# Two decoder layers with adaptive LayerNorm on one core: scores of layer 1 in two passes, and another order of the first loads

## The chip, the core and the metric

The kernel runs on one core of a Trainium2 chip, in fp32. The metric is the device time of one execution in microseconds (us). Each time is a median of several executions; beside it stands one profiled execution, from which all durations are read.

Names of the engines: PE multiplies matrices (PEld are its weight loads), DVE is the vector engine, ACT the activation engine, POOL the general engine, SP issues most transfers (DMA). PE writes its results to PSUM, which has 8 banks of 512 columns here.

## The reference, cut to what matters

The input `x` has 8 sequences of 512 tokens with 256 features. Both layers are of the form below; the two modulations come from small vectors `c` of each sequence.

```python
mod = (_silu(c) @ wmod).reshape(8, 6, 1, -1)          # shift, scale, gate for attention; the same for the FFN
sa, ca, ga, sb, cb, gb = (mod[:, k] for k in range(6))
ga, gb = ...                                          # sign(g) * max(|g|, 0.25)
h = _layernorm(x) * (1 + ca) + sa
x = x + ga * attn(h)
h = _layernorm(x) * (1 + cb) + sb
x = x + gb * ffn(h)
```

Layer 0 attends with a delta rule, a recurrence over the 512 tokens with a 16x16 state for each of the 16 heads (q, k, v are projections with silu; q and k are normalized, beta is a sigmoid). Its FFN sends each token to the best of 8 experts of width 1024. Layer 1 is causal softmax attention with a relative bias, and a weighted mixture of 8 linear experts:

```python
att = q @ k.T / 4 + rel_emb[bucket(i - j)]            # 16 heads of 16 features, causal
y = softmax(att) @ v @ W_proj.T + b_proj
w = softmax(h @ gate_w + gate_b); w = w * (w >= 0.1); w = w / sum(w)
out = sum_e w[:, e] * (h @ expert_w[e] + expert_b[e])
```

## The kernel before

Tokens are cut into four tiles of 128 positions (`NT` = 4); a tile holds the positions of all 8 sequences.

**Setup.** SP loads the constants, then for both layers `cT` and the whole modulation matrix `wm` (1.5 MB each, L107). PE makes shift and scale (L119, both branches) and the gates (L136), DVE forms the gates (L144 to L151), and they are written to DRAM (`mod_d`, L157). The relative bias becomes strips in DRAM (L161 to L169): `strips` (loaded in `load_strips`, L1069) later holds, for each query of a tile and each head, the negative bias of all distances, with 1e30 where the mask cuts.

**Layer 0.** `front(i, at)` makes tile i ready for the scan: `stats(p)` loads tokens of two sequences and takes their statistics (L415 to L424), `normal` and `project(b)` normalize, transpose (L209), project (L447, L451) and apply silu (ACT, L455 to L461), `squares` reduces (L465), `roots` and `scales` form sigmoid, roots and products (POOL, L489), and `heads` transposes K and V to one head per partition (PE L499, ACT copies L502). It returns pieces with the scan step at which each is to be issued. `scan(i, K, V)` is the recurrence: four DVE instructions for each of 128 positions (L536, L540, L546, L551), one position after the other. `run` puts the pieces between the steps: those of the next tile's front, and those of the tile before (`follow`: the rest of attention, routing, expert weights fetched slot by slot). The front of tile 0 runs ahead of the first scan. After the last scan come routing and experts of tile 3, then layer 1.

**Layer 1.** `prologue(b)` makes qT, kT and v of a sequence; `tail(b)` projects, normalizes and applies the experts. Between them runs a loop of steps n (L1330 on): sequence b = n // 16, column c = (n % 16) // 4 (four heads, one on each quarter of PE's rows), query tile i = n % 4.
- `scores(b, c, i)`: four matmuls of 128 queries by the (i+1)*128 keys so far (L1141). For each head DVE adds the strips and takes the minimum of the row in one instruction (L1150, `sc`, `low`; signs are turned, so the minimum is the highest score), and ACT makes the exponentials with it (L1155, `pr`).
- `turn(b, c, j)`, four steps later: PE transposes the exponentials of key tile j (L1167, 16, 12, 8 or 4 blocks), and ACT and DVE copy two heads each to `prT` (L1174, L1176).
- `weigh(b, c, j, prTs)`, one step after that: four matmuls with v (L1188); at j = 3 DVE copies the sums (L1195, `yTc`). v has a column of ones, so that the sums of the exponentials come along.

The order within a step is written in the loop, and each engine takes its instructions in that order:

```python
step = scores(b, m // NT, m % NT)
with tc.issue_after(step):
    last, turned = turned, None
    turned = b, m // NT, m % NT, turn(b, m // NT, m % NT)
    if last:
        weigh(*last)
    while side and side[0][0] < n + 1:
        side.pop(0)[1]()
```

`side` holds the pieces of `prologue(b + 1)` and `tail(b - 1)`, spread over the steps of a sequence. The experts of a tile (L1297 to L1314) are eight matmuls of 512 columns with two expert products each; DVE accumulates them in turn (L1308, eight for a tile), POOL applies the gate and adds the residual (L1312, L1313).

## Time and profile before

| | |
|---|---|
| median of 3 runs | 2357.68 us (2357.12 to 2360.76) |
| the profiled execution | 2365.3 us, span of its instructions 2363.4 us |
| granted PE clock, mean | 0.863 |
| busy: PE, DVE, ACT, POOL | 1772.9, 1604.5, 1076.1, 642.7 us |
| first instruction of the scan | 98.83 us |
| last instruction of the scan | 1153.1 us |
| first scores of layer 1 | 1456.2 us |
| last scores of layer 1 start | 2251.6 us |

The page cuts the span into 40 slices of 59 us; a digit is the busy share in tenths. Lines of the timeline give start, length, engine, line, operation, output and inputs, the number of instructions merged, and in brackets the idle time before with what ended it. In rows by line, the number after x is the count; then come busy time and the mean of one in ns. Line numbers L are those of the kernel before, and in what is said of the changed kernel those of the changed one.

### The profile page before, as it was taken

Reading aid. Unit: us, or ns where it says so; the run is one execution under the profiler, and the core shown is the slowest. Engines: PE = TensorE matmul, PEld = TensorE weight load, DVE = VectorE, ACT = ScalarE, POOL = GpSimd, SP = SyncE. Lnnn points to the kernel's source line nnn. Section 1 sums busy time; section 2 is a strip of 40 time slices with the busy share of each in tenths; the row PEclk is TensorE's granted clock in tenths of the full one; section 3 lists DMA queues with packets and bytes.
Section 4 is the critical chain, followed back from the end, with each engine's and each line's share of the span. In section 5 each row is a group of like instructions: output and inputs, shape, how many; then the busy total and the mean of one; then the engine's idle time right before and its main releaser. Section 6 shows DMA issues by size and latency. Waiting matters only on the chain. (4 is left out here: it accounts for less than half of the span.)

```text
span 2363.4 us, 32128 instructions
## 1 busy us (share of the span) xinstructions
PE 1772.9 (75%) x10874; PEld 1215.8 (51%) x10874; DVE 1604.5 (68%) x4608; ACT 1076.1 (46%) x2579; POOL 642.7 (27%) x796
## 2 busy tenths in 40 slices
PE   6450006569677896869877797999989999999996
PEld 3220004448566685658656685554545454555543
DVE  2499999988998899899651003666666666665653
ACT  3561004455355543523332235774737374646521
POOL 0211006334472544644336633000000101010111
PEclk8675558579888998879977998999999999999997
DMA  5010000057422682248866883000000000000000
GB/s 187 16 47 0 0 0 6 18 193 269 148 72 96 215 290 80 78 168 311 234 115 202 250 299 101 1 4 21 3 21 4 21 3 21 3 21 6 10 10 9
DMA packets 83444, 209.91 MB, mean 89 GB/s; under 512 B 10248, under 2 KB 59568, under 8 KB 67664
## 3 DMA queue, kind: packets, MB, share of 16 engines
q0 software_dynamic: 28848, 157.42, 19.8%
q1 hardware_dynamic: 54432, 50.45, 7.5%
q8 instruction: 86, 1.41, 0.2%
q14 instruction: 78, 0.64, 0.1%
HBM read 175.10 MB, written 32.74 MB: 88 GB/s over the span
## 5 line engine op out<-in xcount | busy, mean ns | idle before, releaser
L1155 ACT ACTIVATE pr<-sc,low 128x384 f32<-128x384 f32 (+3 forms) x512 | 255.8, 556 | 269.5 <-DVE low L1150 267.9
L943 PE MATMUL ps<-hTs,w 128*128 128x128 f32 x1920 | 245.8, 289 | 51.0 <-ACT hTs L935 32.5
L1150 DVE CUSTOM_DVE_ANT_0 sc<-ps,strips 128x384 f32<-128x384 f32 (+3 forms) x512 | 226.6, 485 | 64.6 <-PE ps L1141 51.6
L943 PEld LDWEIGHTS ps<-hTs,w 128*128 128x128 f32 x1920 | 234.3, 203 | 65.4 <-ACT hTs L935 46.6
L540 DVE TENSOR_REDUCE state<-terms 128x16 f32<-128x272 f32 x512 | 227.3, 444 | 15.7
L961 PE MATMUL ps<-w,act 128*128 128x256 f32 x960 | 223.0, 386 | 18.7 <-DMA w<-in_wrows,idx 15.5
L551 DVE TENSOR_TENSOR state<-state,upd 128x256 f32<-128x256 f32 x511 | 220.6, 432 | 17.2
L1303 PE MATMUL ps<-ew,hTd 128*128 128x512 f32 x512 | 230.7, 604 | 0.0
L546 DVE TENSOR_TENSOR upd<-K,state 128x256 f32<-128x256 f32 x511 | 214.0, 419 | 14.9
L536 DVE TENSOR_TENSOR terms<-state,K 128x256 f32<-128x256 f32 x512 | 214.8, 419 | 12.0
L952 ACT ACTIVATE act<-ps,w 128x128 f32<-128x128 f32 x480 | 137.2, 369 | 184.9 <-PE ps L943 108.2
L1308 DVE SCALAR_TENSOR_TENSOR accd<-ps,wtd,accd 128x256 f32<-128x256 f32 x256 | 123.6, 483 | 120.1 <-PE ps L1303 74.3
L961 PEld LDWEIGHTS ps<-w,act 128*128 128x128 f32 x960 | 181.7, 194 | 44.6 <-issue 16.7
L1167 PE MATMUL ps<-cst,pr 128*128 128x128 f32 x1280 | 192.3, 295 | 12.8 <-DVE low L1150 10.6
L1167 PEld LDWEIGHTS ps<-cst,pr 128*128 128x128 f32 x1280 | 148.7, 149 | 87.1 <-issue 35.9
L1312 POOL TENSOR_TENSOR accd<-accd,bc_g 128x256 f32<-128x256 f32 x32 | 23.3, 729 | 559.3 <-DVE accd L1308 559.3
L1303 PEld LDWEIGHTS ps<-ew,hTd 128*128 128x128 f32 x512 | 95.6, 192 | 119.5 <-issue 106.0
L916 POOL DMA_INDIRECT w<-in_wrows,idx x120 | 117.5, 979 | 122.0 <-ACT act L952 90.3
L1141 PE MATMUL ps<-kT,qTc 32*128 32x384 f32 (+3 forms) x1024 | 132.2, 506 | 11.4 <-DVE v L317 6.8
L570 PE MATMUL ps<-cst,V 128*128 128x128 f32 x64 | 13.0, 385 | 169.4 <-DVE V L542 169.4
L636 POOL TENSOR_TENSOR stk<-stk,cst 128x512 f32<-128x512 f32 x96 | 119.3, 1269 | 19.0 <-ACT stk L635 16.9
L1176 DVE COPY prT<-ps 128x512 f32<-128x512 f32 (+3 forms) x256 | 117.7, 483 | 5.0 <-PE ps L1167 4.5
(238 smaller groups left out, 3024.9 us busy)
## 6 DMA issues: line engine op xcount, KB each, us to landing
hs<-zero SPq DMA_DIRECT2D x4, 1920.0 KB
hslot<-hs SPq DMA_DIRECT2D x60, 128.0 KB
ys<-ysb POOLq DMA_DIRECT2D x60, 128.0 KB, 3.8
xt<-in_x SPq DMA_DIRECT2D x16, 256.0 KB
x<-in_x SPq DMA_DIRECT2D x32, 128.0 KB
strips<-strip_d SPq DMA_DIRECT2D x16, 256.0 KB
out<-accd SPq DMA_DIRECT2D x32, 128.0 KB
wm<-in_wmod SPq DMA_DIRECT2D x2, 1536.0 KB
```

The costliest lines, as they stand in the source:

```text
L536: nc.vector.tensor_mul(term[:, :, :HD], M, K[:, s, :].unsqueeze(1).to_broadcast([P, HD, HD]))
L540: nc.vector.tensor_reduce(delta, term, AX.X, ALU.add)
L546: nc.vector.tensor_mul(upd, K[:, s, :].unsqueeze(2).to_broadcast([P, HD, HD]), delta.unsqueeze(1).to_broadcast([P, HD, HD]),)
L551: yield nc.vector.tensor_sub(M, M, upd).ins
L943: nc.tensor.matmul(ph[:, q * P : (q + 1) * P], w[:, k * FF + f * P : k * FF + (f + 1) * P], hT[:, k, :], start=(k == 0), stop=(k == 1),)
L952: nc.scalar.activation(act[:, f, :], ph[:, q * P : (q + 1) * P], AF.Relu, bias=w[:, 2 * FF + f : 2 * FF + f + 1],)
L961: nc.tensor.matmul(py[:, :D], act[:, f, :], w[:, f * D : (f + 1) * D], start=(f == 0), stop=(f == NFC - 1),)
L1141: made = nc.tensor.matmul(pscs[r][:, :W], qT[rows, g, o, i * P : (i + 1) * P], kT[rows, g, :W], start=True, stop=True,)
L1150: nc.vector.tensor_tensor_reduce(out=sc[:, :W], in0=pscs[r][:, :W], in1=strips[:, n, S - W :], scale=1.0, scalar=3.0e38, op0=ALU.add, op1= ...
L1155: nc.scalar.activation(pr, sc[:, :W], AF.Exp, bias=low, scale=-1.0)
L1167: nc.tensor.transpose(pt[:, (i - j) * P : (i - j + 1) * P], prs[r, i][:, j * P : (j + 1) * P], ident,)
L1303: nc.tensor.matmul(pe, hT[:, k, cols], ew[:, k, e : e + 2, :], start=(k == 0), stop=(k == 1),)
```

## The change

**Setup and layer 0.** The block ahead of layer 0 goes. The modulation matrix is loaded in four parts (layer, branch); the first comes right after the constants, then the tokens of tile 0 (`x_first`, in the room of K), then `wqkv`, then the other three parts and the buckets. Shift and scale of layer 0's attention are made first. The rest of the modulation (`shift_scale`, with ACT copies), the gates (`gate_rows`: ACT copy, four DVE instructions on 8x256, POOL's DMA), the strips (`strip_rows`: now two kinds, POOL's DMAs), the product of the output weights and the loads of the gates become pieces of the first scan, at its steps 2 to 26. The front of tile 1 starts at step 30 of that scan (before: 2). In tile 0, `stats_first` takes all statistics with one square root, `turn(b)` is apart from `project(b)` and ahead of it, `roots` and `scales` run once for all eight sequences, DVE takes some of the products, and DVE makes half of the copies in `heads`.

**Layer 1.** `scores` keeps matmul and reduction and only leaves the minima (`lows`), in columns that the transpose puts at a row of q that meets a constant 1 in k. `highest` (one step later) transposes them (L1305) and subtracts them from q: for i = 3 on DVE from PSUM, otherwise ACT negates and POOL adds. `exps` then multiplies k by q again, the other way round (keys by queries, L1324), DVE adds transposed strips (L1332, `stripsT`, 4 MB loaded when layer 0's room is free) and ACT makes the exponentials in place (L1333). There is no transpose of exponentials and no copy. In the loop the order is `scores`, `highest` of the step before, `weigh` of the step before, side pieces, `exps`. k is kept in two masked copies, v is packed 20 columns a head. In `experts`, DVE accumulates two of the eight products; for the other six ACT scales and POOL adds. The copies `yTc` and `wT` move from DVE to ACT.

The diff, cut to its core:

```diff
+        def load_mod(layer, branch):
+            if branch == 0:
+                nc.sync.dma_start(
+                    cTs[layer], t[f"cT{layer}"].rearrange("(k p) b -> p k b", p=P)
+                )
+            wm = fp.tile([P, 2, 3 * D], F32, tag=f"w{branch}", name=f"wm{layer}{branch}", bufs=2)
+            cols = slice(3 * D * branch, 3 * D * (branch + 1))
+            nc.sync.dma_start(
+                wm, t[f"wmod{layer}"][:, cols].rearrange("(k p) m -> p k m", p=P)
+            )
+            wms[layer, branch] = wm
...
+        def gate_rows(layer, branch):
+            wm = wms[layer, branch]
+            pg = bank()
+            for k in range(2):
+                nc.tensor.matmul(
+                    pg[:B, :D], scs[layer][:, k, :], wm[:, k, 2 * D :],
+                    start=(k == 0), stop=(k == 1),
+                )
+            name = f"{layer}{branch}"
+            g, sign, mag, gt = (
+                fp.tile([B, D], F32, tag=tag, name=f"{tag}_{name}", bufs=2)
+                for tag in ("hslot", "yrow", "ysb", "hTs")
+            )
+            nc.scalar.copy(g, pg[:B, :D])
+            nc.vector.tensor_scalar(sign, g, 0.0, 2.0, ALU.is_ge, ALU.mult)
+            nc.vector.scalar_tensor_tensor(mag, g, -1.0, g, ALU.mult, ALU.max)
+            nc.vector.tensor_scalar_max(mag, mag, 0.25)
+            nc.vector.scalar_tensor_tensor(gt, sign, -1.0, mag, ALU.add, ALU.mult)
+            nc.gpsimd.dma_start(mod_d[f"g{name}"], gt)
...
+        load_mod(0, 0)
+        for p in range(B // 2):
+            nc.sync.dma_start(
+                x_first[:, 2 * p : 2 * p + 2],
+                t["x"][2 * p : 2 * p + 2, :P, :].rearrange("b p d -> p b d"),
+            )
         nc.sync.dma_start(wqkv, t["wqkvT0"].rearrange("(k p) m -> p k m", p=P))
+        shift_scale(0, 0)
+        for layer, branch in ((0, 1), (1, 0), (1, 1)):
+            load_mod(layer, branch)
+        load_buckets()
...
+            def stats_first():
+                mv = room[:, 1, : 2 * B].rearrange("p (b s) -> p b s", s=2)
+                sd, rs, off = (room[:, 1, k * B : (k + 1) * B] for k in (2, 3, 4))
+                for b in range(B):
+                    st = ep.tile([P, 6], F32, tag="sta", name=f"st_first{b}", bufs=2)
+                    nc.vector.bn_stats(st, x_first[:, b, :])
+                    nc.vector.bn_aggr(mv[:, b, :], st)
+                nc.scalar.activation(sd, mv[:, :, 1], AF.Sqrt, bias=ln_eps)
+                nc.vector.reciprocal(rs, sd)
+                nc.vector.scalar_tensor_tensor(
+                    off, mv[:, :, 0], -1.0, rs, ALU.mult, ALU.mult
+                )
+                for p in range(B // 2):
+                    bs = slice(2 * p, 2 * p + 2)
+                    got[p] = x_first[:, bs], rs[:, bs], off[:, bs]
...
+                        ve = nc.vector if i == 0 and which and b % 2 else nc.gpsimd
+                        ve.tensor_mul(view, view, by.unsqueeze(2).to_broadcast([P, NH, HD]))
...
+                    if i == 0 and d0 % 8:
+                        nc.vector.tensor_copy(to, pt.rearrange("p (d t) -> p d t", d=4))
+                    else:
+                        nc.scalar.copy(to, pt.rearrange("p (d t) -> p d t", d=4))
...
+            else:
+                pieces = [
+                    (2, weights0),
+                    (4, lambda: shift_scale(0, 1)),
+                    (6, lambda: gate_rows(0, 0)),
+                    (8, lambda: gate_rows(0, 1)),
+                    (10, lambda: shift_scale(1, 0)),
+                    (12, lambda: shift_scale(1, 1)),
+                    (14, lambda: gate_rows(1, 0)),
+                    (16, lambda: gate_rows(1, 1)),
+                    (18, lambda: strip_rows(0)),
+                    (20, lambda: strip_rows(1)),
+                    (26, load_gates),
+                ]
...
-                parts, more = front(i + 1, 47 if i > 0 else 2)
+                parts, more = front(i + 1, 47 if i > 0 else 30)
...
         def scores(b, c, i):
-            kT, qT, prs = got[b]["kT"], got[b]["qT"], got[b].setdefault(c, {})
+            kT, qT = got[b]["kT"], got[b]["qT"]
             g, o = c // 2, c % 2
             W = (i + 1) * P
             pscs = [bank() for _ in range(4)]
             for r in range(4):
                 rows = slice(32 * r, 32 * r + 32)
                 made = nc.tensor.matmul(
-                    pscs[r][:, :W], qT[rows, g, o, i * P : (i + 1) * P], kT[rows, g, :W],
+                    pscs[r][:, :W], qT[rows, g, o, i * P : (i + 1) * P], kT[rows, g, o, :W],
                     start=True, stop=True,
                 )
+            at = HD * (1 - o)
             for r in range(4):
                 n = 8 * g + 2 * r + o
-                sc = lp.tile([P, S], F32, tag="sc", name=f"sc{b}_{i}_{n}", bufs=4)
-                low = lp.tile([P, 1], F32, tag="low", name=f"low{b}_{i}_{n}", bufs=8)
+                sc = lp.tile([P, S], F32, tag="sc", name=f"sc{b}_{i}_{n}", bufs=1)
                 nc.vector.tensor_tensor_reduce(
                     out=sc[:, :W], in0=pscs[r][:, :W], in1=strips[:, n, S - W :],
-                    scale=1.0, scalar=3.0e38, op0=ALU.add, op1=ALU.min, accum_out=low,
-                )
-                pr = lp.tile([P, W], F32, tag=f"pr{i}", name=f"pr{b}_{i}_{n}", bufs=6)
-                nc.scalar.activation(pr, sc[:, :W], AF.Exp, bias=low, scale=-1.0)
-                prs[r, i] = pr
+                    scale=1.0, scalar=3.0e38, op0=ALU.add, op1=ALU.min,
+                    accum_out=lows[:, o, i % 2, r, at : at + 1],
+                )
             return made.ins
-        def turn(b, c, j):
-            prs = got[b][c]
+        def highest(b, c, i):
+            g, o = c // 2, c % 2
+            pt = bank()
+            nc.tensor.transpose(
+                pt[:, :P], lows[:, o, i % 2].rearrange("p r e -> p (r e)"), ident
+            )
+            q = got[b]["qT"][:, g, o, i * P : (i + 1) * P]
+            if i == NT - 1:
+                nc.vector.tensor_sub(q, q, pt[:, :P])
+                return
+            high = lp.tile([P, P], F32, tag="high", name=f"high{b}_{c}_{i}")
+            nc.scalar.mul(high, pt[:, :P], -1.0)
+            nc.gpsimd.tensor_add(q, q, high)
+        def exps(b, c, j):
+            kT, qT = got[b]["kT"], got[b]["qT"]
+            g, o = c // 2, c % 2
             W = S - j * P
+            pscs = [bank() for _ in range(4)]
+            for r in range(4):
+                rows = slice(32 * r, 32 * r + 32)
+                nc.tensor.matmul(
+                    pscs[r][:, :W], kT[rows, g, o, j * P : (j + 1) * P], qT[rows, g, o, j * P :],
+                    start=True, stop=True,
+                )
             prTs = []
             for r in range(4):
-                pt = bank()
-                for i in range(j, NT):
-                    nc.tensor.transpose(
-                        pt[:, (i - j) * P : (i - j + 1) * P],
-                        prs[r, i][:, j * P : (j + 1) * P],
-                        ident,
-                    )
+                n = 8 * g + 2 * r + o
                 prT = lp.tile([P, S], F32, tag="prT", name=f"prT{b}_{c}_{j}_{r}", bufs=8)
-                if r % 2:
-                    nc.scalar.copy(prT[:, :W], pt[:, :W])
-                else:
-                    nc.vector.tensor_copy(prT[:, :W], pt[:, :W])
+                nc.vector.tensor_add(prT[:, :W], pscs[r][:, :W], stripsT[:, n, :W])
+                nc.scalar.activation(prT[:, :W], prT[:, :W], AF.Exp, scale=-1.0)
                 prTs.append(prT)
             return prTs
...
+                sums = lp.tile([P, D], F32, tag="sumd", name=f"sumd{b}_{i}")
+                nc.scalar.copy(sums, pb[:, :D])
                 acc = lp.tile([P, D], F32, tag="accd", name=f"accd{b}_{i}")
-                nc.scalar.copy(acc, pb[:, :D])
                 for e in range(0, NE, 2):
                     pe = bank()
                     for k in range(2):
...
                             start=(k == 0), stop=(k == 1),
                         )
                     for j in range(2):
-                        nc.vector.scalar_tensor_tensor(
-                            acc, pe[:, j * D : (j + 1) * D], wt[:, i, e + j : e + j + 1], acc,
-                            ALU.mult, ALU.add,
-                        )
+                        part, by = pe[:, j * D : (j + 1) * D], wt[:, i, e + j : e + j + 1]
+                        if (e, j) == (0, 0):
+                            nc.vector.tensor_scalar(acc, part, by, None, ALU.mult)
+                        elif (e, j) == (4, 0):
+                            nc.vector.scalar_tensor_tensor(
+                                acc, part, by, acc, ALU.mult, ALU.add
+                            )
+                        else:
+                            term = lp.tile(
+                                [P, D], F32, tag="term", name=f"term{b}_{i}_{e + j}", bufs=2
+                            )
+                            nc.scalar.activation(term, part, AF.Copy, scale=by)
+                            nc.gpsimd.tensor_add(sums, sums, term)
+                nc.gpsimd.tensor_add(acc, acc, sums)
...
-                last, turned = turned, None
+                if 0 < n <= B * STEP:
+                    b, m = divmod(n - 1, STEP)
+                    highest(b, m // NT, m % NT)
+                if made:
+                    weigh(*made)
+                while side and side[0][0] < n + 1:
+                    side.pop(0)[1]()
+                made = None
                 if NT <= n < B * STEP + NT:
                     b, m = divmod(n - NT, STEP)
-                    turned = b, m // NT, m % NT, turn(b, m // NT, m % NT)
-                if last:
-                    weigh(*last)
-                while side and side[0][0] < n + 1:
-                    side.pop(0)[1]()
+                    made = b, m // NT, m % NT, exps(b, m // NT, m % NT)
```

## The prediction

> **What bounds the kernel now.** I read the slices of the page first, then busy time by stage, then the timeline of the stage that is long.
>
> ```profile
> span 2363.4 us, 32128 instructions
> ...
> PE   6450006569677896869877797999989999999996
> ...
> DVE  2499999988998899899651003666666666665653
> ...
> PEclk8675558579888998879977998999999999999997
> ```
>
> One slice is 59 us. DVE is full from slice 2 to 18 (layer 0's scan) and PE from slice 25 to 38 (layer 1). In between the FFN of the last token tile streams its weights, started by the end of the scan.
>
> ```profile
> 1456.20:2251.60 795.40, 737.72 (x4406) 409.95 (x4410) 513.86 (x1828) 479.95 (x1061) 80.31 (x109) 0.96 0.05 13
> 98.80:1152.50 1053.70, 651.89 (x4314) 524.43 (x4315) 960.13 (x2436) 424.43 (x1077) 387.57 (x469) 0.79 0.35 119
> ```
>
> These rows give, for two stretches, the length, then the busy time of PE, weight loads, DVE, ACT and POOL, then PE's clock. In layer 1, PE is busy 93% and DVE 65%; in the scan DVE is busy 91%. So three things set the end: when the scan starts (98.8 us), its DVE time, and PE's order in layer 1. Four steps of layer 1 on PE:
>
> ```profile
> 1775.51 1.97 PE L1167 MATMUL ps<-cst,pr 128*128 128x128 f32 x16 [0.16 <-ACT prT L1174]
> 1777.40 0.43 PE L1188 MATMUL ps<-prT,v 128*32 128x128 f32 x8
> ...
> 1779.65 0.71 PE L1141 MATMUL ps<-kT,qTc 32*128 32x256 f32 x8
> 1780.29 1.53 PE L1167 MATMUL ps<-cst,pr 128*128 128x128 f32 x12
> 1781.75 1.06 PE L1188 MATMUL ps<-prT,v 128*32 128x512 f32 x8
> 1782.75 1.13 PE L313 MATMUL ps<-wqkv,hTc 128*128 128x256 f32 x4
> ...
> 1785.11 0.93 PE L1141 MATMUL ps<-kT,qTc 32*128 32x384 f32 x8
> ...
> 1790.18 1.20 PE L1141 MATMUL ps<-kT,qTc 32*128 32x512 f32 x8
> ```
>
> A step is scores (L1141), transposes of the exponentials (L1167), weighing of the *previous* step's transposes (L1188), then side work (here L313 and what follows). Between the transposes of a step and their weighing lie its side work, the next scores and the next transposes: the copies L1174 and L1176 have some 5 us, and PE hardly ever waits for them. From the start of scores to the first side matmul the four steps take 3.57, 3.10, 2.92 and 3.25 us: **12.84 us for one c**, of which there are 32.
>
> **Layer 1: the steps after.** In the built program PE's order becomes: transposed scores of step n (L1324), scores of n+1 (L1285), one transpose of minima (L1305), weighing of n (L1345), side work, transposed scores of n+1. Weighing now needs what was made just before it: four DVE adds (L1332) and four exponentials (L1333), with only one set of scores as cover; behind the waiting L1345 stand the side work and the next transposed scores, so all of PE. The chain, for widths 512, 384, 256, 128:
> - first result after the matmuls start: 1.16, 0.95, 0.74 (first L1150 after the L1141 starts above: 1791.34, 1786.06, 1780.39), and 0.63 (1456.24 to 1456.87);
> - three more adds, priced as the reductions L1150, which also read PSUM and strips (start to start 0.60, 0.47, 0.345, 0.21): 1.80, 1.42, 1.04, 0.63; the last add's own time 0.69, 0.55, 0.42, 0.29;
> - hand-overs, an estimate: 0.1; the last exponential (L1155 by shape) 0.72, 0.61, 0.50, 0.40;
> - the last weighing, two passes, each as long as one of L1303 (7.06 us for 16 of width 512): 0.90, 0.67, 0.45, 0.25.
>
> Sums: 5.4, 4.3, 3.25, 2.3, or **15.2 us for one c**, against 12.84: +2.4 us x 32 = **+76 us**. If the weighing's two passes of the last tile lay wholly beside other matmuls, it would be 1.1 less for a c: +40.
>
> What PE alone would need: 12.84, less the transposes (start to start 1.89, 1.46, 1.08, 1.04), plus a second set of scores (0.60, 0.64, 0.86, 1.13), plus four transposes at 0.2: 11.4 us. So PE's own work does get shorter, by 1.4 us for a c; it doesn't get to use it.
>
> The other engines, for one of 8 batches. DVE: adds 16 x (0.60+0.47+0.345+0.21) = 26 us and 4 subtractions at 0.3 come; copies (73 us in 550 us, five batches: 14.6), 24 accumulations L1308 at 0.48 (11.6) and the copies of yTc and wT (3.5) go: about -2.5 us. ACT: 24 terms at 0.38, yTc 2.3, negations 12 x 0.25, wT 0.6 and second halves of kT 2.8 come, 12.1 of copies go: +5.7 of 110 us, with ACT at 60% hidden behind PE; uncovered it would be +45 in all. POOL gets 28 additions at 0.73 in expert pieces: with the two old ones nine for a tile, 6.6 us beside PE's 7.7 us for a tile (2341.13 to 2348.82), hidden; where ACT's last term waits for POOL, up to 1 us for each of 32 tiles. The 12 additions of q on POOL have a step of time. The square roots: 15 visits with two table loads of 1.28 us each now stand in the queue ahead of exponentials that PE waits for; from 0 to 15 x 2.9 = 43; I take +10, since the second load can lie beside the adds. At the start, the second strips wait for the last multiplication with the gates (1456 us) and their first quarter, 1 MB, for some 5 us at the 177 GB/s of that stretch, beside the first four scores (SP issues all 32 loads of them ahead of the next batch's tokens, which have until step 6); then the minimum, its transpose and subtraction stand ahead of the first exponentials: +4. At the end ACT and POOL finish the last tile in place of two accumulations: +2 (4 additions of 0.73 less 0.96).
>
> PE will wait 1 us a step, up to 2.3 us; what is its clock then? After a wait of 3.94 us at 1767 us the next scores took 2.09 us instead of 1.20; after one of 1.13 us at 1796.5 us the sixteen transposes took 2.20 instead of 1.97. I price it at 0, by the nearer row; above it, the row of the last 112 us has a clock of 0.89 with PE busy 81%: some 78 us of PE work for a batch x 8 x (0.96/0.89 - 1) = +49. [...]
>
> [...]
>
> **The start.** The scan's first instruction is at 98.83 us. Before it:
>
> ```profile
> 10.60 6.96 PE L119 MATMUL ps<-sc,wm 128*128 128x8 f32 x32 [10.60 <-DMA wm<-in_wmod]
> ...
> 34.18 0.69 PE L209 MATMUL ps<-cst,xna 128*128 128x128 f32 x2 [5.14 <-ACT xna L206]
> ...
> 90.53 3.68 PE L499 MATMUL ps<-cst,qk 128*128 128x128 f32 x16 [10.64 <-POOL qk L489]
> ...
> 98.83 0.38 DVE L532 TENSOR_TENSOR terms<-state,V 128x128 f32<-128x128 f32 x1 [13.47 <-ACT V L502]
> ```
>
> After: 0.39 MB of constants, 0.79 of modulation, 1.05 of tokens, 0.80 of wqkv on one queue, at the 221 GB/s of the first 20 us and 2.5 us before the first lands: modulation 7.8, tokens 12.6, wqkv 16.2 us. Statistics are 0.51 us for each batch, all but the last pair ahead of the last tokens; with root, normalizing and transposes the first projection starts at 16.5 rather than 35.4. A batch costs PE 1.98 + 1.08 + 0.38 = 3.44 us at the fast durations, 3.78 + 2.02 + 0.69 = 6.5 at the slow ones that follow waits; eight of them, one to two slow: 32.5, so to 49 (before 5.8 us for each, with six changes of tables between). From the last projection to the scan it was 18.4 us. POOL's K products now stand after four others and not after eight (-2.5), ACT and DVE share the copies (-1), one reciprocal is twice as wide (+1): 16, with one reduction ahead of it: scan start at 66 to 67. **-32 us**; bounds -24 (tokens in 1 KB rows at half the rate) and -38 (all batches fast).
>
> In the scan DVE gets 16 operations on 8x256 (the 8x512 rows are 0.41, 0.67, 0.41, 0.68; I take two thirds, 1.4 for a gate) and 0.75 for the output weights: **+6**, nothing hides it, as DVE is the bound there; not below +3. The rest (small matmuls, ACT copies, POOL's DMAs of gates and strips, SP's two gate loads) finds engines that are idle half the time; the next tile's front moves from step 2 to 30 and ends at 79 of 128. What follows the scan hangs on its end, so the -26 goes through to layer 1.
>
> **Sum.** +76 +10 +4 +2 -32 +6 = +66 us. The profiled execution took 2365.3 us (span 2363.4), 7.6 above the median of 2357.7; I carry the difference over to the median: **2424 us**. Its own range: 2375 (overlapped last weighing, no root stalls) to 2495 (part of the clock, roots and POOL at their upper ends).
>
> **Rivals.**
> - *The chain is covered, and PE's shorter work counts* (faster). Place: the wait ahead of L1345. Against it: the built order, and DVE's 0.60 us for each add. For it: 15.2 is a sum of parts of which the first result and the last weighing may overlap more. It decides at (26 - 16)/32 = 0.3 us above 12.84, so 13.1 us for a c; fully covered, 11.4 x 32 gives -46 - 26 + 6: 2292 us. Chance 0.22, spread from 2285 to 2353.
> - *PE's clock falls too*, with table loads on top: +49 and more, 2475 to 2530. For it the rows of 1767 us; against it that waits of 1 us left durations alone. Beyond 2495: 0.07.
> - *The first loads don't come earlier*, because tokens and modulation share the engines: -24 in place of -32, 2432; inside the range. 0.08.
>
> The forecast has 0.63, all within 2353 to 2495. The range 2310 to 2495 leaves out some 0.1 below and 0.07 above. A difference of 0.2% is about what a measurement can tell from none: faster 0.22, same 0.03, slower 0.75.
>
> **What would show it.** Right: a scan start near 67 us; in layer 1 PE idle ahead of L1345, put down to ACT's prT (L1333), of 0.5 to 2 us in each step, PE busy under 90%, steps of 6.8 us rather than 6.26. Wrong: PE busy 95% with steps under 6.1 us; or waits that stand at L1324 (for q from POOL) or L1305; or a clock under 0.92.

## The result and the profile after

The changed kernel takes 2499.0 us (median of 4 runs, 2495.06 to 2505.87); the kernel before, beside it, 2359.2 us. The ratio is 1.059, with a 95% interval of 1.0555 to 1.0625: slower by 140 us, where the forecast was slower by 66. The profiled execution took 2505.9 us.

The slices of the page after:

```profile
span 2503.8 us, 32578 instructions
...
PE   5142065696778777689678779999899898989996
...
DVE  3999999889977998993300176646464656465631
...
PEclk8676576798889997799789879999999999999997
```

DVE fills up one slice earlier; PE is at 8 or 9 tenths in layer 1 as before, and its clock stays at 9 there. By these digits nothing is wrong with PE. The stages, as before: length, then busy time of PE, weight loads, DVE, ACT and POOL, then the clock. They are layer 1 from the first to the last scores, the rest of it, the scan, and what lies between scan and layer 1:

```profile
1436.20:2377.30 941.10, 859.94 (x4282) 406.17 (x4283) 551.25 (x1923) 474.68 (x1085) 242.78 (x371) 0.94 0.07 15
2377.30:2503.80 126.50, 100.80 (x322) 44.71 (x318) 29.76 (x96) 46.14 (x108) 58.17 (x81) 0.86 0.03 10
64.66:1126.70 1062.04, 656.85 (x4355) 526.06 (x4354) 963.86 (x2457) 427.33 (x1087) 390.18 (x475) 0.80 0.35 120
1126.70:1436.20 309.50, 241.04 (x1654) 205.98 (x1654) 54.92 (x148) 102.58 (x309) 143.85 (x169) 0.87 0.68 201
```

and the end of layer 1 in the kernel before:

```profile
2251.60:2363.40 111.80, 90.83 (x326) 45.52 (x322) 50.45 (x134) 21.09 (x49) 17.39 (x24) 0.89 0.03 10
```

The scan starts 34 us earlier and layer 1 starts 20 us earlier; the steps of layer 1 take 941 us where they took 795, and the end 126.5 where it took 111.8. Two steps on PE (start, length, engine, line, operation, operands, number, and in brackets the idle time before with its releaser):

```profile
1828.14 1.14 PE L1324 MATMUL ps<-qTc,kT 32*128 32x512 f32 x8
1829.11 0.67 PE L1285 MATMUL ps<-kT,qTc 32*128 32x256 f32 x8
1830.73 0.33 PE L1305 MATMUL ps<-cst,lows 128*128 128x128 f32 x1 [0.95 <-DVE prT L1332]
1831.49 2.81 PE L1345 MATMUL ps<-prT,v 128*32 128x512 f32 x8 [0.42 <-DVE prT L1332]
1834.23 1.13 PE L263 MATMUL ps<-wqkv,hTc 128*128 128x256 f32 x4
...
1836.59 0.93 PE L1324 MATMUL ps<-qTc,kT 32*128 32x384 f32 x8
1837.34 1.72 PE L1285 MATMUL ps<-kT,qTc 32*128 32x384 f32 x8
1839.48 0.33 PE L1305 MATMUL ps<-cst,lows 128*128 128x128 f32 x1 [0.43 <-DVE prT L1332]
1839.74 2.12 PE L1345 MATMUL ps<-prT,v 128*32 128x384 f32 x8
1841.79 1.13 PE L263 MATMUL ps<-wqkv,hTc 128*128 128x256 f32 x4
```

The weighing of width 512 takes 2.81 us, where the same eight matmuls took 1.06 before: they stand and wait for one exponential after the other, 0.62 us apart, and the profile counts part of that as busy. So the busy share of PE (91%) hides what it was to show. The cycle of these two steps, from L1324 to the first side matmul (L263), is 6.1 and 5.2 us; 5.4 and 4.3 were forecast. What DVE does meanwhile:

```profile
1829.66 0.43 DVE L125 BATCH_NORM_STATS2 std<-xs 128x6 f32<-128x256 f32 x1 [0.69 <-POOL xs L1404]
1830.00 0.67 DVE L1332 TENSOR_TENSOR prT<-ps,stripsT 128x512 f32<-128x512 f32 x1
1830.59 0.17 DVE L126 BATCH_NORM_AGGREGATE mvd<-std 128x2 f32<-128x6 f32 x1
1830.68 1.85 DVE L1332 TENSOR_TENSOR prT<-ps,stripsT 128x512 f32<-128x512 f32 x3
1832.45 0.41 DVE L1294 CUSTOM_DVE_ANT_0 sc<-ps,strips 128x256 f32<-128x256 f32 x1
...
1833.02 0.42 DVE L1294 CUSTOM_DVE_ANT_0 sc<-ps,strips 128x256 f32<-128x256 f32 x1
...
1833.60 0.42 DVE L1294 CUSTOM_DVE_ANT_0 sc<-ps,strips 128x256 f32<-128x256 f32 x1
```

Two things were not in the forecast. A statistic of the tail (L125, mean and variance of a tile's rows) stands in DVE's queue ahead of the adds and waits there 0.69 us for POOL's xs. And the reductions, 0.42 us long, start 0.575 us apart; before they started 0.345 apart:

```profile
1780.39 0.41 DVE L1150 CUSTOM_DVE_ANT_0 sc<-ps,strips 128x256 f32<-128x256 f32 x1
...
1780.73 0.42 DVE L1150 CUSTOM_DVE_ANT_0 sc<-ps,strips 128x256 f32<-128x256 f32 x1
```

They now all write the one tile `sc` (before: four). The reading, which experiment A tests, is that each waits until the one ahead has written; no row of waits names this.

The start, on PE:

```profile
7.89 3.56 PE L356 MATMUL ps<-room,wm 128*128 128x8 f32 x16 [7.89 <-DMA wm<-in_wmod]
16.61 1.18 PE L148 MATMUL ps<-cst,xna 128*128 128x128 f32 x4 [5.16 <-ACT xna L145]
17.85 3.68 PE L544 MATMUL ps<-wqkv,hT 128*128 128x512 f32 x4
...
57.43 3.68 PE L605 MATMUL ps<-cst,qk 128*128 128x128 f32 x16 [12.37 <-POOL qk L597]
```

and the first instruction of the scan, on DVE:

```profile
64.66 0.38 DVE L646 TENSOR_TENSOR terms<-state,V 128x128 f32<-128x128 f32 x1
```

Modulation at 7.9 us, first projection at 17.9, scan at 64.7: forecast were 7.8, 16.5 and 66 to 67.

### The profile page after: what moved, and what is told of

It is laid out like the page before. It is cut to its first block, busy times and chain, and to the rows that moved or that the text cites. A ratio compares the mean times of both kernels' runs of the same rounds, so it can differ in the third digit from the quotient of the medians.

```text
span 2503.8 us, 32578 instructions
## 1 busy us (share of the span) xinstructions
PE 1895.7 (76%) x10748; PEld 1208.2 (48%) x10748; DVE 1621.8 (65%) x4668; ACT 1085.3 (43%) x2660; POOL 848.1 (34%) x1118
## 5 line engine op out<-in xcount | busy, mean ns | idle before, releaser
L1332 DVE TENSOR_TENSOR prT<-ps,stripsT 128x256 f32<-128x256 f32 (+3 forms) x512 | 219.4, 481 | 126.5 <-PE ps L1324 111.9
L1294 DVE CUSTOM_DVE_ANT_0 sc<-ps,strips 128x384 f32<-128x384 f32 (+3 forms) x512 | 249.1, 487 | 50.3 <-PE ps L1285 5.7
L1333 ACT ACTIVATE prT<-prT 128x256 f32<-128x256 f32 (+3 forms) x512 | 215.7, 467 | 124.5 <-DVE prT L1332 117.6
L1075 PE MATMUL ps<-w,act 128*128 128x256 f32 x960 | 224.5, 388 | 16.7 <-DMA w<-in_wrows,idx 12.6
L1345 PE MATMUL ps<-prT,v 128*32 128x512 f32 (+3 forms) x1024 | 214.3, 470 | 19.1 <-ACT prT L1333 12.2
L1314 POOL TENSOR_TENSOR qTc<-qTc,high 128x128 f32<-128x128 f32 x96 | 43.6, 454 | 498.6 <-ACT high L1313 498.6
L1285 PE MATMUL ps<-kT,qTc 32*128 32x128 f32 (+3 forms) x1024 | 186.9, 495 | 14.0 <-DVE lows L1294 8.7
L1480 POOL TENSOR_TENSOR sumd<-sumd,term 128x256 f32<-128x256 f32 x192 | 139.1, 725 | 171.9 <-ACT term L1479 165.9
L1479 ACT ACTIVATE term<-ps,wtd 128x256 f32<-128x256 f32 x192 | 84.8, 471 | 164.4 <-DVE accd L1470 78.5
L1285 PEld LDWEIGHTS ps<-kT,qTc 32*128 32x128 f32 x1024 | 103.7, 200 | 75.8 <-DVE prT L1332 25.5
```

The costliest lines, as they stand in the source:

```text
L1075: nc.tensor.matmul(py[:, :D], act[:, f, :], w[:, f * D : (f + 1) * D], start=(f == 0), stop=(f == NFC - 1),)
L1285: made = nc.tensor.matmul(pscs[r][:, :W], qT[rows, g, o, i * P : (i + 1) * P], kT[rows, g, o, :W], start=True, stop=True,)
L1294: nc.vector.tensor_tensor_reduce(out=sc[:, :W], in0=pscs[r][:, :W], in1=strips[:, n, S - W :], scale=1.0, scalar=3.0e38, op0=ALU.add, op1= ...
L1332: nc.vector.tensor_add(prT[:, :W], pscs[r][:, :W], stripsT[:, n, :W])
L1333: nc.scalar.activation(prT[:, :W], prT[:, :W], AF.Exp, scale=-1.0)
L1345: nc.tensor.matmul(yT[32 * r : 32 * r + 32, j * P :], v[:, j, (4 * c + r) * VW : (4 * c + r) * VW + 32], prTs[r][:, :W], start=(j == 0), s ...
```

## The experiments

Four candidates for the time lost in layer 1: **A**, the spacing of the reductions; **B**, the chain add, exponential, weighing that PE waits for; **C**, the experts' sum on ACT and POOL; **F**, the statistics in DVE's queue. In all runs "layer 1" is the time from the first scores to the end in the profiled execution: 907.2 us before (795.4 + 111.8), 1067.6 after (941.1 + 126.5). Each is from one execution; the old layer 1 took 907.2 and 905.7 us in two kernels, so a difference of a few us tells little. Ratios are to the kernel before, run beside each on the same chip. A wait given for a line is that of its matmuls and their weight loads together, as the view of the line has it; PE may be at work on others during part of it.

| kernel | ratio, 95% interval | layer 1, us |
|---|---|---|
| before | 1 | 907.2 |
| changed | 1.059 [1.0555, 1.0625] | 1067.6 |
| new start, old layer 1 | 0.9875 [0.983, 0.992] | 905.7 |
| A: two scratch tiles | 1.045 [1.038, 1.051] | 1043.3 |
| B: side work first | 1.044 [1.039, 1.050] | 1044.8 |
| C: experts' sum on DVE | 1.050 [1.045, 1.055] | 1057.1 |
| F: statistics behind the adds | 1.050 [1.046, 1.054] | 1050.1 |
| A + B | 1.025 [1.023, 1.028] | 985.0 |
| A + B + C | 1.011 [1.009, 1.013] | 965.6 |
| A + B + C, second pass a step later | 1.017 [1.013, 1.021] | 968.1 |
| A + C, weighing a step later | 1.008 [1.005, 1.011] | 967.7 |
| A + B + C + F | 1.000 [0.997, 1.003] | 942.7 |
| changed, no adds in the second pass | 1.024 [1.021, 1.027] | 994.7 |
| A + B + C, no adds | 0.983 [0.978, 0.987] | 901.0 |

**The start alone.** Setup and layer 0 of the changed kernel, with `prologue`, `scores`, `turn`, `weigh`, the experts and the loop as they were before (here against the changed kernel):

```diff
-                nc.vector.tensor_add(prT[:, :W], pscs[r][:, :W], stripsT[:, n, :W])
-                nc.scalar.activation(prT[:, :W], prT[:, :W], AF.Exp, scale=-1.0)
+                if r % 2:
+                    nc.scalar.copy(prT[:, :W], pt[:, :W])
+                else:
+                    nc.vector.tensor_copy(prT[:, :W], pt[:, :W])
...
-                    made = b, m // NT, m % NT, exps(b, m // NT, m % NT)
+                    turned = b, m // NT, m % NT, turn(b, m // NT, m % NT)
+                if last:
+                    weigh(*last)
```

> The new start of layer 0 (quarter of the modulation first, tokens second, the rest and both strips in scan steps) with layer 1 as it was before. All theories: the scan starts near 65 us in place of 98.8 and ends some 27 us earlier, and a layer 1 that is not changed keeps these 27: 2326 to 2340 us against 2359 before. Nearer to 2359: the start's gain is given back between the scan and layer 1, and the layer 1 of the change costs less than it seems. The distance from this run to the changed kernel (about 165 us if 2333) is what the two-pass scores cost as a whole.

Measured: 2334.6 us, ratio 0.9875, some 30 us gained; layer 1 took 905.7 us, as before.

```profile
1417.00:2210.60 793.60, 736.65 (x4408) 408.79 (x4410) 514.02 (x1828) 479.92 (x1061) 80.17 (x109) 0.96 0.05 13
```

So the start's gain is kept, and the two-pass layer 1 costs 165 us by itself. This version is faster than both kernels, and the fastest here of those that compute the whole reference.

**A: the spacing of the reductions.**

```diff
-                sc = lp.tile([P, S], F32, tag="sc", name=f"sc{b}_{i}_{n}", bufs=1)
+                sc = lp.tile([P, S], mybir.dt.bfloat16, tag="sc", name=f"sc{b}_{i}_{n}", bufs=2)
```

> The changed kernel with two scratch tiles for the reductions in place of one (16 bits wide, so that both fit where one was; nothing reads them). Theory A, spacing: four reductions that write one tile wait for each other, which is 0.23 us each, 512 in all or 118 us of VectorE, and lies on the chain from scores to highs to exponentials: starts of the reductions go back from 0.84/0.70/0.575/0.445 us apart to about 0.60/0.47/0.345/0.21, and the time falls by 50 to 110 us, to 2390 to 2450. Rival B, chain: the wait of the weighing for the exponentials sets the step and the reductions have slack: within 15 us of 2499. Rival C, experts: as B.

Measured: ratio 1.045, layer 1 24 us shorter. Reductions of width 256 on DVE:

```profile
1705.57 0.41 DVE L1294 CUSTOM_DVE_ANT_0 sc<-ps,strips 128x256 bf16<-128x256 f32 x1
...
1705.91 0.42 DVE L1294 CUSTOM_DVE_ANT_0 sc<-ps,strips 128x256 bf16<-128x256 f32 x1
...
1706.25 0.42 DVE L1294 CUSTOM_DVE_ANT_0 sc<-ps,strips 128x256 bf16<-128x256 f32 x1
```

They start 0.34 us apart again and are no shorter themselves, so the second tile did it and not the narrower type; three tiles of 32 bits (in A + B + C) give 0.345 as well. The cause is real; the size was expected at two to four times as much. The 118 us of the expectation count 512 gaps; a batch of four reductions has three, so 88 us at most, and only 24 of them stood in the path while PE waited for the exponentials anyway (117 us ahead of L1345 in both kernels).

**B: the chain's cover.**

```diff
-                if made:
-                    weigh(*made)
                 while side and side[0][0] < n + 1:
                     side.pop(0)[1]()
+                if made:
+                    weigh(*made)
```

> The changed kernel with the side work of a step ahead of the weighing on TensorE, so that about two pieces of it lie beside the way from the adds to the exponentials. Theory B, chain: the 117 us that TensorE waits at L1345 for prT fall below 60, and the time falls by 50 to 120 us, to 2380 to 2450. Rival A, spacing: VectorE is late with the adds by its queue (reductions, then the side's operations), so the wait only moves to the banks (transposes of the highs and the side's matmuls waiting for VectorE's prT): 2470 to 2515. Rival C, experts: as A.

Measured: ratio 1.044, layer 1 23 us shorter. The wait for exponentials ahead of L1345 fell from 117.0 to 19.8 us, more than expected, and layer 1 by less than half of the 50 us that were the least expected. Other waits grew: at the scores (L1285) for banks that the adds free from 26.9 to 63.6 us, and at L1345 itself 20.5 us came in for the experts' terms on ACT (L1479; 1.1 at most in the changed kernel). And PE's clock fell; first the row of all steps, then three stretches:

```profile
1420.10:2341.20 921.10, 806.37 (x4280) 395.42 (x4283) 550.65 (x1923) 473.30 (x1085) 244.77 (x372) 0.87 0.07 16
1540.00:1560.00 20.00, 17.01 (x113) 10.14 (x109) 14.54 (x51) 10.10 (x25) 4.14 (x7) 0.84 0.00 1
1555.00:1560.00 5.00, 5.00 (x16) 3.15 (x19) 3.01 (x11) 1.83 (x5) 0.45 (x1) 0.50 0.00 0
1560.00:1580.00 20.00, 18.52 (x123) 9.34 (x115) 12.49 (x47) 15.49 (x33) 2.36 (x4) 0.98 0.03 8
```

In the 20 us from 1540 on the longest wait of PE was 1.62 us (it ended at 1553.84), and the clock was 0.84; in the 5 us from 1555 on PE was busy throughout and the clock was 0.50. Over all steps it was 0.87, against 0.94 in the changed kernel, where much of PE's waiting lay within the weighing. What lowers the clock there is not shown by these rows.

**C: the experts' sum.**

```diff
...
-                            nc.scalar.activation(term, part, AF.Copy, scale=by)
-                            nc.gpsimd.tensor_add(sums, sums, term)
-                nc.gpsimd.tensor_add(acc, acc, sums)
+                        nc.vector.scalar_tensor_tensor(
+                            acc, pe[:, j * D : (j + 1) * D], wt[:, i, e + j : e + j + 1], acc,
+                            ALU.mult, ALU.add,
+                        )
```

> The changed kernel with the experts' sum on VectorE alone as it was before (8 operations of 0.42 us per tile in place of two, no terms on ScalarE and no sums on GpSimd). Theory C, experts: terms of 0.47 us stand among the exponentials on ScalarE, and GpSimd's sums hand xs to the next batch late: the time falls by 20 to 60 us (2440 to 2480), the tail after the last scores goes from 126 us back to about 113. Rivals A and B: VectorE takes 192 more operations, 80 us busy, and is the engine that is late: the time rises by 5 to 40 us (2505 to 2540), only the tail gains some 12.

Measured: ratio 1.050, some 21 us by the ratios and at the low end of what was expected; layer 1 by itself is 10.5 us shorter, although DVE is busier in it by 90 us. The tail only went from 126.5 to 123.8 us, so that part was wrong: the last tile's sum on ACT and POOL is not what made the end longer. The traces show where most of it lies. In the changed kernel, over several engines:

```profile
1937.14 0.72 POOL L1483 TENSOR_TENSOR accd<-accd,xs 128x256 f32<-128x256 f32 x1
...
1938.33 1.81 SPq L256 DMA_DIRECT2D xs<-x  x4
...
1941.11 0.43 DVE L125 BATCH_NORM_STATS2 stc<-xs 128x6 f32<-128x256 f32 x1 [3.13 <-DMA xs<-x]
...
1943.98 0.69 PE L1387 MATMUL ps<-cst,yc 128*128 128x128 f32 x2 [5.86 <-DVE yc L1377]
```

SP issues the next sequence's tokens (L256) behind the store of an experts' tile (at 1937.89 us), which waits for POOL's sum; DVE stands at their statistic, with `yc` (L1377) behind it in its queue, and PE waits for `yc`. PE's matmuls waited 29.4 us for `yc` in the changed kernel, 20.4 with C, and 21.9 in the kernel before.

**A and B together, then C, then the second pass later.** A + B is both edits; the next adds C (with three tiles `sc` of 32 bits); the last also has

```diff
-                if NT <= n < B * STEP + NT:
-                    b, m = divmod(n - NT, STEP)
+                if NT < n <= B * STEP + NT:
+                    b, m = divmod(n - NT - 1, STEP)
```

> The changed kernel with both edits: two scratch tiles for the reductions, and the side work ahead of the weighing. Alone they took 24 and 23 us from layer 1 (first scores to end: 1067.6 us in the changed kernel, 1043.3 and 1044.8 with the one or the other). Theory A and B together, two causes in one chain: with the side work ahead of the weighing what is left to wait for is VectorE's adds (transposes of the highs and scores wait for banks), and shorter spacing brings just these forward: 50 to 85 us in all, layer 1 at 985 to 1018, 2415 to 2450 us. Rival, one slack counted twice: whichever is cured first leaves the other nothing: 22 to 35 us in all, layer 1 at 1033 to 1045, 2465 to 2480.

> As the kernel with both edits, and the experts' sum back on VectorE (the scratch tiles are then three of 32 bits). Alone the third edit took 10 us from layer 1, and none from its tail. Theory C adds: 8 to 25 us less than with two edits. Rival: with the spacing cured VectorE is what sets the step, and 80 us more of work on it cost 5 to 30 us against the two edits.

> As the kernel with three edits, with the second pass one step later, so that the highs of a c have a step more to reach q before the first exponentials need them. Theory D, the highs' route (transpose, ScalarE's negation or VectorE's subtraction, q) stands in the path once per c: 0.5 to 1 us for each of 32 c's, so 15 to 32 us less than with three edits. Rival: other work stands there already: within 8 us of it.

Measured: A + B took 82.6 us from layer 1 (at the upper end of what was expected), where A and B alone took 24.3 and 22.8. So with the exponentials covered the spacing counts for more: PE's waits for the reductions ahead of L1285, L1305 and L1324 are 34.4 us here and 60.0 in B alone. The expected way, that the adds free their banks sooner, doesn't show: the waits for these were 63.6 us at L1285 and 67.7 at L1305 in B alone, and are 68.8 and 65.6 here. The clock is likely the larger part: it was 0.87 in B alone and is 0.92 here.

```profile
1429.10:2297.30 868.20, 766.14 (x4283) 375.46 (x4284) 524.27 (x1923) 472.58 (x1085) 244.45 (x372) 0.92 0.07 17
```

With PE 806 us busy at 0.87 in B alone, the step to 0.92 is worth 806 x (1 - 0.87/0.92) = 44 us, an estimate; the surplus of both over the sum of each is 35.5. Of the 53 us between the steps of B alone (921.1) and these (868.2), 40 lie in PE's busy time for the same matmuls (806.4 and 766.1), which fits; a part of that can be blocked matmuls that read as busy, and the two were not told apart. C took 19 us more, within what was expected: PE's matmuls waited 33.0 us for `yc` with A + B and 22.1 with C, and the 20.5 us at L1345 for ACT's terms are gone. The second pass a step later did not help (965.6 and 968.1 us, ratios 1.011 and 1.017), so by these runs the way from the minima to q has slack.

**The weighing a step later.** In place of B, with A and C; the tiles for the exponentials become as narrow as their step needs, four sets of them:

```diff
-        side, made = [], None
+        side, made = [], []
...
-                if made:
-                    weigh(*made)
+                if len(made) > 1 or n > B * STEP + NT:
+                    weigh(*made.pop(0))
```

> The changed kernel with two scratch tiles, the experts' sum on VectorE, and (in place of the side work ahead of the weighing) the weighing one step later: the exponentials then have a whole step, since the tiles for them are as narrow as each step needs and so there are four sets. Theory B, chain: another cover for the same wait does what the first did: no wait at L1345 for the exponentials, layer 1 within 20 us of the 965.6 us of the kernel with three edits, 2375 to 2410 us. Rival: the gain of the three edits came from the side work's place between scores and weighing, and not from the wait: layer 1 near 1025 us (1067.6 less 24 less 19), 2440 to 2465 us.

Measured: layer 1 at 967.7 us, 2 us from A + B + C. Another cover for the same wait does the same, so it was the wait and not the place of the side work that B cured.

**Without the adds.** The relative bias and the mask are left out of the second pass:

```diff
-                nc.vector.tensor_add(prT[:, :W], pscs[r][:, :W], stripsT[:, n, :W])
-                nc.scalar.activation(prT[:, :W], prT[:, :W], AF.Exp, scale=-1.0)
+                nc.scalar.activation(prT[:, :W], pscs[r][:, :W], AF.Exp, scale=-1.0)
```

> The changed kernel without the second pass's adds on VectorE: ScalarE takes its exponentials straight from the banks, so the relative bias and the mask are left out of the second pass. Theory B, chain: 512 adds of 0.28 to 0.67 us (219 us of VectorE) leave the chain, of which at least the first of a step (0.6/0.47/0.345/0.21, 52 us in all) stands alone in it: 60 to 150 us less, 2350 to 2440. Rival, TensorE itself or its clock sets the step: within 20 us of 2499.

> The kernel with three edits without the second pass's adds (relative bias and mask are left out of the second pass; ScalarE takes the exponentials straight from the banks). Of the three edits' layer 1 (965.6 us, 58 more than before) TensorE waits 110 us for banks that these adds free. Theory E, banks: without the adds layer 1 comes to 895 to 925 us, 2310 to 2350 us in all, as the old layer 1 or under it. Rival: TensorE's own work with its short matmuls sets what is left: 945 to 965 us, 2370 to 2390 us.

Measured: 73 us less of layer 1 in the changed kernel, 65 us less with A, B and C:

```profile
1413.00:2204.30 791.30, 726.20 (x4283) 356.56 (x4284) 406.81 (x1577) 383.02 (x943) 122.59 (x204) 0.94 0.09 18
```

Only without its second pass over PSUM does DVE let the two-pass layer 1 be as short as the old one, 901 to 907 us. The adds are what the three edits leave uncovered; a part of it comes back below with F. Whether it is their time in the chain or the banks that they hold, this edit doesn't tell: it takes away both.

**F: the statistics.** Their DVE instructions are queued behind the last add of the step that their tile was projected in:

```diff
...
-                stats.update(enumerate(row_stats("d", [xs[:, i, :] for i in range(NT)])))
...
+                    with tc.issue_after(adds[min(due[i], len(adds) - 1)]):
+                        nc.vector.bn_stats(st, xs[:, i, :])
+                        nc.vector.bn_aggr(mv[:, i, :], st)
```

> The changed kernel with the tail's statistics (L125, four for a sequence) queued on VectorE behind the adds of their step in place of among them. Theory F, queue: in the steps at 1828 to 1846 us of the changed kernel a statistic stands ahead of or between the four adds, waits 0.69, 0.45 and 0.62 us for GpSimd's xs and takes 0.35 itself; these steps took 6.1, 5.2 and 4.3 us against 5.4, 4.3 and 3.25 forecast. Three such steps in each of 7 sequences, 0.8 to 1.0 us each: 17 to 21 us less, layer 1 near 1048 us, 2476 to 2486 us. Rival: the weighing waits for ScalarE's exponentials or VectorE's reductions a little later all the same: within 8 us of 2499.

> As the kernel with three edits (two or more scratch tiles, side work ahead of the weighing, experts' sum on VectorE), and the statistics behind the adds of their step. There VectorE waits 36 us for GpSimd's xs ahead of statistics, with banks held meanwhile. Theory F: 15 to 35 us less than with three edits, layer 1 at 930 to 950 us, 2355 to 2375 us: the two-pass scores would then be within a per cent of the kernel before, with the earlier start in it. Rival: the waits move to the banks of the next step: within 8 us of 2390.

Measured: 17.5 us less of layer 1 in the changed kernel (17 to 21 expected), 23 us less with A, B and C.

```profile
1817.46 1.42 DVE L1334 TENSOR_TENSOR prT<-ps,stripsT 128x256 f32<-128x256 f32 x4 [0.27 <-PE ps L1326]
1818.84 0.43 DVE L1415 BATCH_NORM_STATS2 std<-xs 128x6 f32<-128x256 f32 x1
```

The four adds are together, and the statistic no longer waits. With all four edits:

```profile
1430.20:2253.60 823.40, 749.02 (x4283) 366.94 (x4284) 590.42 (x2068) 408.61 (x941) 121.63 (x203) 0.94 0.08 18
2253.60:2372.90 119.30, 96.45 (x324) 45.02 (x318) 52.46 (x144) 24.83 (x60) 17.85 (x25) 0.81 0.03 10
```

The whole kernel then takes what the kernel before takes (ratio 1.000, 0.997 to 1.003). The start's 30 us pay for what the two passes still cost: layer 1 is 35 us longer than the old one.

## Why the prediction was right or wrong

Right in sign and in the wait that bounds the step; the size was off by 74 us, since the prediction gave no time to what else stands in the queues of DVE and POOL. The measured 2499 us lie above its range (to 2495). By its own steps, in the profiled executions:

| step of the prediction | forecast, us | measured, us |
|---|---|---|
| scan starts earlier | -32 | -34.2 |
| the scan, longer by DVE's insertions | +6 | +7.5 (1054.3 to 1061.8) |
| from the scan's end to layer 1 | 0 | +6.7 |
| steps of layer 1: chain +76, roots +10, start +4 | +90 | +145.7 |
| after the last scores | +2 | +14.7 |

- **The start was right in total**, and the run with the start alone shows that it goes through to the end. Its parts were not, and that they cancel is luck: the eight projections took 27 us (17.85 to 45.06) for 32.5 forecast, and from the last of them to the scan it was 19.6 us for 16. That way was 18.9 us before, not 18.4, and did not get shorter: PE waits 12.37 us there for POOL's products, where it waited 10.64. The bound of -24 put the tokens at half the rate, which no run shows: over the first 20 us all transfers together moved 300 GB/s, where 221 were forecast, and the last two statistics of the tokens began at 14.20 us. The 6.7 us between scan and layer 1 are not shown to belong to the change: with one and the same layer 0, the first scores came between 1413 and 1436 us in the kernels above.
- **"Steps of 6.8 us" failed: they took 7.4.** The mechanism stood: weighing right behind its exponentials is what PE waits for (117 us ahead of L1345; two different covers each take that wait away). The failing step is the chain's middle part, the adds "priced as the reductions" back to back, with the rest of DVE at "about -2.5 us" for a batch and no order among its instructions. In the four steps from 1823.7 us on the chain came to 18.1 us for 15.2 forecast: 6.1, 5.2, 4.3 and 2.5 for widths 512, 384, 256 and 128, where 5.4, 4.3, 3.25 and 2.3 were forecast. In the first three a statistic stood among the adds, with waits of 0.69, 0.45 and 0.62 us and 0.35 of its own each. With the statistics behind the adds (F) the same four steps took 5.3, 4.3, 3.3 and 2.7, or 15.6 us; there the working of the chain was right. The 0.1 us for hand-overs in it was the author's estimate, from no row of the kernel before; in the changed kernel the first exponentials of widths 512 and 384 start 0.04 and 0.03 us after their adds end (at 1830.71 and 1838.13 us). Over the whole of layer 1 the way from L1324 to the first side matmul took 5.8, 4.6, 3.9 and 2.8 us in the mean, or 17.1 for a c (for the 27 to 29 steps of each width that have side work ahead of the next L1324): 1.9 x 32 = 61 us over the forecast, an estimate, where the steps took 56 us more. F is worth 17.5 us of that. The trace of the kernel before had shown the sign, among the reductions of the steps that the forecast priced:

```profile
1787.08 0.43 DVE L186 BATCH_NORM_STATS2 std<-xs 128x6 f32<-128x256 f32 x1 [0.46 <-POOL xs L1246]
```

- **Reductions were taken as unchanged.** The diff says `bufs=1` for `sc`, and the prediction has no term for it. It cost 24 us alone, and 60 beside B (82.6 - 22.8), where the clock rose with it.
- **"POOL hidden, ACT hidden" failed** by 10 us alone (19 beside A and B); the bound that the prediction gave, up to 1 us for each of 32 tiles, holds it, but for another reason: not ACT's terms waiting for POOL, but POOL's last sum, which puts off the load of the next sequence's tokens and with it `yc` (9 us of PE's waits, see C).
- Together: 17.5 + 24.3 + 10.5 = 52 us of the 68 that layer 1 took above the forecast of +92. These were measured one by one against the changed kernel, and the edits don't simply add, so this is a sum of sizes and no proof that nothing else is in it. The square roots were not tried by themselves.
- **The end: +2 failed.** From the last scores to the first transposes after the last weighing (L1372, before L1214) it now takes 56.5 us and took 43.7, 12.8 of the 14.7 us. The last four second passes run there without scores beside them, each with its whole chain; that this is the cause is a reading, which the 116.8 us of the end with A + B support. The prediction had priced the end by the experts' last tile alone, and C showed that this was not it.
- **"Clock under 0.92" did not come**: 0.94 and 0.86 against 0.96 and 0.89 before. By the prediction's own form the fall from 0.96 to 0.94 is worth at most 860 x (1 - 0.94/0.96) = 18 us, an estimate, and less as far as PE's busy time is waiting; it was priced at 0 and may be a part of the 16 us that A, C and F leave open. (The 78 us of PE work for a batch in the +49 stand in no row: 737.7 us in 8 batches, less 1.4 for each of four c's, are 86, which gives +54.) The rival of a falling clock is real: it showed in B alone (0.87 over the steps).
- **The rival "PE's shorter work counts"** (2292 us) can't be had by covering the chain. With the chain covered in two ways layer 1 was 966 and 968 us; with the adds left out as well 901; the forecast for it was 907 - 46 = 861.

Of the tests that the prediction named, the main one came out: 117 us ahead of L1345 are 0.9 us a step. Two gave wrong signs. "PE busy under 90%" read 91%, since blocked weighings count as busy; and waits at L1305 (76.5 us for the adds, 16.7 for the minima) were to mean that the theory was wrong, though they are the same adds, seen by the next instruction that needs a bank.

## What to carry to other kernels

When a change puts a short chain between engines into every step, list all that stands in the queue of each engine of the chain, and of the DMA queue that feeds it, in the built order, with what each of these waits for; add that to the chain before anything is called hidden. Look at the number of buffers of a tile that is written and never read: here one buffer in place of two spaced its writers out and cost 24 us. And take a change with two independent parts apart at once: here one part alone was worth 1.25%, and the other cost 7%.

## What the runs showed of the hardware

- Reductions on DVE that write the same tile one after the other start 0.22 to 0.23 us further apart than those with a tile each: 0.43, 0.575, 0.705 and 0.84 us for widths 128 to 512 in the changed kernel, against 0.21, 0.345, 0.48 and 0.61 before. At width 256 it is 0.34 with two tiles and 0.345 with three. By these rows a tile that is written again at once has a price here; that it is a wait for the write ahead is a reading that no row of waits names.
- PE's clock does not go by its busy share alone: with PE busy 88% of the steps it was 0.87 in B alone and 0.92 in A + B, and with 93% it was 0.96 in the kernel before and 0.93 in F alone. In a 20 us stretch of 0.84 in B alone the longest wait was 1.62 us. That the form of the waits makes the difference is a guess of the author's and not shown.
- Blocked matmuls read as long ones: 2.81 us for the eight weighings of width 512 in the changed kernel, which took 1.06 before.
